# Local attention on Trainium2: scores of one head on half of TensorE's rows, softmax maxima for two pairs at once in two PSUM banks, and a ring of four banks for the rest

## The chip, the cores and the metric

The kernel runs on one core of a Trainium2 chip. A core has TensorE (PE in the profile, with its weight loads as PEld), VectorE (DVE), ScalarE (ACT), GpSimd (POOL) and SyncE (SP), which here issues the DMAs. Each engine has its own queue and takes its instructions in the order in which they were issued to it; the engines meet through semaphores. TensorE writes its results to PSUM, which this kernel divides into eight banks of 128 partitions x 512 float32 values; VectorE and ScalarE read and write PSUM and SBUF.

The metric is device microseconds of one launch. The kernel before took 4397.36 us (median of three runs, 4397.0 to 4401.22).

## The reference, cut to what matters

The program is a chain of eight layers on 8 sequences of 256 tokens with 128 features: a selective state space model, a local transformer block, an attention over tokens, the same local block a second time, a linear attention, a four-bit feed-forward, a head attention and the four-bit feed-forward again. The change lies in the local block alone, which runs twice. It has six layers (DEPTH = 6), and each has an attention and a feed-forward part with residual additions:

```python
HEADS, DIM_HEAD, WINDOW = 16, 64, 32
def attn_layer(x, Wqkv, qs, ksc, Wo):
    q, k, v = (sh(t) for t in split(x @ Wqkv, 3))       # (b, 16 heads, 256, 64)
    q, k = l2norm(q) * qs, l2norm(k) * ksc
    q = q * cos * scale + rotate_half(q) * sin * scale
    k = k * cos / scale + rotate_half(k) * sin / scale
    # a window of 32 queries sees its own 32 keys and the 32 before
    sim  = einsum('bhwie,bhwje->bhwij', bq, look(bk)) * 8.0
    sim  = where(mask, -finfo.max, sim)                 # 32 x 64 per window
    attn = softmax(sim, -1)
    out  = einsum('bhwij,bhwje->bhwie', attn, look(bv))
    return out @ Wo
def ffn_layer(x, g, bln, W1, b1, W2, b2):
    a, gate = split((layernorm(x) * g + bln) @ W1 + b1, 2)
    return (a * gelu(gate)) @ W2 + b2
```

All of it is float32.

## The kernel before, in words

The data are worked on transposed (features on partitions) in four chunks `c` of two sequences, so 512 tokens at a time. A chunk in a layer is a unit; six layers of four chunks make 24 units, and the 16 heads of a unit go as eight pairs `p` = 0 to 7. `LocalBlock.steps` (L607) writes the whole order by hand: one step `i` for each pair of each unit, and in a step one call for each stage, some for a later pair and some for an earlier one. No scheduler changes it. The stages of a step, in the order in which they are issued to every engine's queue:

- `rotate` (pair i+6): two GpSimd operations of 128x1024, L367 and L368; the first waits for the DMA that swaps the halves of a head.
- `prep` (pair i+1): a matmul spreads the key norms over the partitions (L410), and VectorE multiplies keys by them into a buffer `kb` (L414), twice, once for each head of the pair, with a column `hcol` that is one on the rows of that head and zero on those of the other.
- `share` (pair i-1, odd pairs only): VectorE's softmax sums of two pairs and their reciprocals (L460, L461).
- `project` (pair i+7): six matmuls make q and k in two PSUM banks (L213 to L215); ScalarE copies each bank out (L338), VectorE multiplies it by a table (L340) after ScalarE's read of the same bank, two DMAs from SP's queue swap the halves (L343, L344), ScalarE squares (L348).
- `rounded`, `shared` (GpSimd, L469: probabilities times reciprocals), then side work (weight loads of the next layer: `load_qk`, `load_v`, `load_1`), `norms` and `norms_end` (VectorE L377, three ScalarE operations L131 to L134, VectorE L142 and L146), and a piece of `feed`, the feed-forward of the unit one and a half units behind: eight pieces, at pairs 4 to 7 the layer norm, at 0 the gate, at 2 the other half, at 3 the output matmuls (L563).
- `attended`, `turn` (odd pairs: transposes of the probabilities into two banks, L482, copied by ScalarE, L485).
- `scores` (pair i): 16 matmuls (L429), then four VectorE operations on the bank (L437 to L440): times the query norms, plus the mask, the maxima, and the subtraction into SBUF.
- `values` (32 matmuls, L325, into two banks, copied by ScalarE, L327), `attend` (odd pairs, L505), `squares` (L359), and last `soft` (odd pairs: ScalarE's exponential of two pairs at once, L450).

In the program a float32 matmul is one call; the trace shows most of them as two instructions, each with a weight load of its own.

A row block of 128 holds both heads of a pair, first halves of both, then second halves (rows 0 to 31 are head 0, 32 to 63 head 1, 64 to 95 head 0, 96 to 127 head 1). So a score matmul runs over all 128 rows and makes both heads' scores side by side, 2 x 64 columns, from the two masked copies in `kb`. The four windows of a group go to four column tiles of 32, that is, to four blocks of 32 output partitions.

PSUM banks are given out in turn. `K.bank` (L121) takes the next bank of a named list, and whoever gets a bank again waits for the last reader of its former contents:

```python
RING, NRM, ACC = "012345", "6", "7"      # L38
```

The ring of six serves `prep` (one bank), `project` (two), `scores` (one), `values` (two), `turn` (two in odd steps), the feed-forward (ten in a unit), `attended`, `rounded` and the weight loads.

Of the kernel before, what the change touches and what calls it, by code (L numbers as in the profile page):

```python
# [10 lines left out]
F32 = mybir.dt.float32  # L11
# [10 lines left out]
NCH = 4  # L22
CT = 512
# [14 lines left out]
RING, NRM, ACC = "012345", "6", "7"  # L38
# [5 lines left out]
def f32(ap):  # L44
    return ap.bitcast(F32)
# [172 lines left out]
class LocalBlock:  # L218


    def __init__(self, k):
# [5 lines left out]
        self.mask = k.const(P, "c_mask", (128, 512), BF)  # L227
        self.hcol = k.const(P, "c_hcol", (128, 2))
# [9 lines left out]
        self.zero = P.tile([32, 128], BF, name="zero")  # L238
        self.kb = [P.tile([128, 2, 32 + CT], F32, name="kb_%d" % i) for i in range(NKB)]
# [12 lines left out]
        for t in self.rs:  # L252
            nc.vector.tensor_scalar(t, self.mask, 0.0, None, ALU.mult)
# [75 lines left out]
    def project(self, u, p):  # L329
# [13 lines left out]
        nc.sync.dma_start(out=sw[0:64], in_=raw[64:128])  # L343
        nc.sync.dma_start(out=sw[64:128], in_=raw[0:64])  # L344
# [61 lines left out]
    def prep(self, u, p):  # L406
# [6 lines left out]
        for h in range(2):  # L413
            nc.vector.scalar_tensor_tensor(kb[:, h, 32:], tt[:, 1], self.hcol[:, h:h + 1], rb, ALU.mult, ALU.mult)  # L414
        u.kb[p] = kb

    def scores(self, u, p):


        k, P, nc = self.k, self.P, self.k.nc  # L420
        mm = nc.tensor.matmul
        kb = u.kb.pop(p)
        qf = u.t.pop(p)[:, 0]
        sp = k.bank(RING)
        s4 = sp.rearrange("p (o a j) -> p a o j", o=2, a=8)
        for wg in range(4):
            for w in range(4):
                win = 4 * wg + w
                mm(s4[32 * w:32 * w + 32, 2 * wg:2 * wg + 2], qf[:, 32 * win:32 * win + 32],  # L429
                   kb[:, :, 32 * win:32 * win + 64].rearrange("p h (o j) -> p h o j", o=2),  # L430
                   start=True, stop=True)
        mx = P.tile([128, 8], F32, name="mx", tag="mx", bufs=2)
        if p % 2 == 0:
            u.pr = P.tile([128, 2, 8, 2, 32], F32, name="pr", tag="pr", bufs=NPR)
        pr = u.pr
        rq = u.rq[p // GP][:, p % GP].rearrange("p w h -> p (w h)")
# [5 lines left out]
        if p % 2:  # L442
            u.prs[p] = pr
# [1052 lines left out]
```

## Time and profile before

| what | value |
|---|---|
| median of three runs | 4397.36 us |
| the profiled execution | 4402.16 us, span 4400.4 us, mean granted TensorE clock 0.922 |
| first and last score matmul of the first local block | 630.2 us to about 2195 us |
| the same of the second | 2435 us to about 4015 us |
| score matmuls L429 | 12288 instructions, 418.6 us busy, mean 277 ns |
| VectorE on the scores, L437 to L440 | 4 x 384 operations of 128x512, 694, 700, 691 and 691 ns |
| VectorE, keys times norms, L414 | 768 operations of 128x512, 741 ns |
| ScalarE, exponential L450 | 192 operations of 128x1024, 1061 ns |
| SP's swap DMAs, L343 and L344 | 768 of 256 KB, median 3.5 us from issue to landing |

The span is the time from the first to the last instruction of the profiled execution, and busy time is the union of an engine's instructions. [...] An "idle before" figure is the time for which the engine stood still ahead of a group of instructions, with the operation that ended it.

In the trace one can follow the steps by the first score matmul of each. In a unit in which no weights are loaded, one step after the other takes 5.88, 10.07, 9.84, 8.06, 6.39, 8.77, 6.27 and 8.80 us, 64.1 us in all, the same to 0.05 us from layer to layer. The three other units of a layer take about 66, 69 and 66 us.

### The profile page before, as it was taken

How to read it: one execution, taken by the hardware profiler on the slowest of the kernel's cores; microseconds unless marked ns; L12 is line 12 of the kernel's file. 1: busy time of each engine (PE TensorE's matmuls, PEld its weight loads, DVE VectorE, ACT ScalarE, POOL GpSimd, SP SyncE). 2: the span in 40 equal slices, each digit the busy share in tenths (PEclk: the TensorE clock that was granted, in tenths of full speed). 3: DMA queues.
4: the chain of work that ended last, by engine and by line, in shares of the span. 5: the costliest groups of instructions: out<-in, count | busy, mean ns of one | idle time of the engine just before them, and what ended most of it. 6: DMA issues, size and time to landing. Idle time of an engine off the chain costs nothing.

```text
span 4400.4 us, 147972 instructions
## 1 busy us (share of the span) xinstructions
PE 3760.2 (85%) x64201; PEld 2852.7 (65%) x64201; DVE 3705.8 (84%) x5687; ACT 2645.0 (60%) x5050; POOL 3078.2 (70%) x1546
## 2 busy tenths in 40 slices
PE   5656679999999999999966899999999999997376
PEld 2222257777778778777744777787787777775144
DVE  6999958888888888888876788888888888887988
ACT  5423347767667677677544676676676767764322
POOL 3656668878778778787575887787877877862433
PEclk7777889999999999999966999999999999998578
DMA  0000033323233233333202332232333323221000
GB/s 19 7 3 16 1 78 81 89 74 89 72 75 90 73 85 74 78 82 76 54 20 68 81 90 72 69 93 72 88 74 74 87 71 92 72 71 42 15 6 10
DMA packets 134900, 272.97 MB, mean 62 GB/s; under 512 B 31020, under 2 KB 68328, under 8 KB 134248
## 3 DMA queue, kind: packets, MB, share of 16 engines
q1 hardware_dynamic: 134248, 263.51, 23.9%
q8 instruction: 503, 8.24, 0.8%
q14 instruction: 149, 1.22, 0.1%
HBM read 49.50 MB, written 6.29 MB: 13 GB/s over the span
## 4 chain that ended last, share of the span: by engine, by line
DVE 38%; PE 37%; ACT 13%; issue 8%; POOL 2%; DMA 2%; SPq 0%; DVEq 0%; POOLq 0%; ACTq 0%
PE pb L505 6%; PE pb L325 5%; DVE big L340 4%; DVE big L816 4%; DVE big L414 4%; PE pb L429 3%; DVE big L460 3%; PE pb L563 3%; PE pb L359 3%; DVE pb L438 2%; DVE big L439 2%; PE pb L410 2%; DVE pb L437 2%; DVE big L440 2%; ACT big L348 2%
## 5 line engine op out<-in xcount | busy, mean ns | idle before, releaser
L367 POOL TENSOR_TENSOR big<-big 128x1024 f32<-128x1024 f32 x384 | 916.0, 2385 | 405.0 <-DMA big<-big 319.7
L368 POOL TENSOR_TENSOR big<-big 128x1024 f32<-128x1024 f32 x384 | 917.2, 2389 | 30.1
L325 PE MATMUL pb<-big 128*32 128x128 f32 x24576 | 748.8, 274 | 4.3 <-DVE big L301 4.0
L414 DVE SCALAR_TENSOR_TENSOR big<-big,pb 128x512 f32<-128x512 f32 x768 | 537.7, 741 | 193.7 <-PE pb L410 153.3
L325 PEld LDWEIGHTS pb<-big 128*32 128x32 f32 x24576 | 681.6, 111 | 12.9 <-DVE big L301 7.1
L327 ACT COPY big<-pb 128x512 f32<-128x512 f32 x768 | 439.1, 597 | 317.8 <-PE pb L325 316.0
L338 ACT COPY big<-pb 128x512 f32<-128x512 f32 x768 | 440.1, 585 | 280.3 <-PE pb L215 248.6
L340 DVE TENSOR_TENSOR big<-pb,big 128x512 f32<-128x512 f32 x768 | 482.6, 668 | 43.6 <-ACT big L338 43.0
L469 POOL TENSOR_TENSOR big<-big 128x1024 f32<-128x1024 f32 x192 | 365.6, 1904 | 217.2 <-ACT big L348 133.6
L348 ACT ACTIVATE big<-big 128x512 f32<-128x512 f32 x768 | 443.4, 629 | 0.0
L505 PE MATMUL pb<-big 128*32 128x128 f32 x11520 | 402.0, 278 | 43.8 <-ACT big L485 35.0
L817 POOL TENSOR_TENSOR big<-big 128x1024 f32<-128x1024 f32 x128 | 305.3, 2398 | 191.4 <-DVE big L816 186.3
L213 PE MATMUL pb<-bigr 128*128 128x512 f32 (+1 forms) x1056 | 429.6, 407 | 11.3 <-ACT bigr L298 8.9
L215 PE MATMUL pb<-bigr 128*128 128x512 f32 (+1 forms) x1056 | 422.0, 400 | 4.2 <-DVE bigr L299 3.7
L429 PE MATMUL pb<-big 128*32 128x128 f32 x12288 | 418.6, 277 | 7.7 <-DVE big L440 4.7
L214 PE MATMUL pb<-bigr 128*128 128x512 f32 (+1 forms) x1056 | 420.1, 398 | 1.0 <-POOL bigr L203 1.0
L505 PEld LDWEIGHTS pb<-big 128*32 128x32 f32 x11520 | 325.3, 111 | 107.2 <-ACT big L485 91.4
L429 PEld LDWEIGHTS pb<-big 128*32 128x32 f32 x12288 | 314.9, 110 | 110.0 <-ACT big L338 32.7
L810 PE MATMUL pb<-bigr 128*128 128x512 f32 x512 | 214.0, 533 | 181.2 <-DVE big L816 124.6
L437 DVE TENSOR_TENSOR pb<-pb,big 128x512 f32<-128x512 f32 x384 | 266.4, 694 | 69.7 <-PE pb L429 67.3
L450 ACT ACTIVATE big<-big 128x1024 f32<-128x1024 f32 x192 | 203.7, 1061 | 191.5 <-DVE big L440 179.1
L359 PE MATMUL pb<-big 128*32 128x128 f32 x6144 | 296.4, 275 | 19.2 <-DVE big L146 8.6
(270 smaller groups left out, 7400.6 us busy)
## 6 DMA issues: line engine op xcount, KB each, us to landing
big<-big SPq DMA_DIRECT2D x768, 256.0 KB, 3.5
big<-in_wqk SPq DMA_DIRECT2D x96, 128.0 KB, 3.4
big<-x SPq DMA_DIRECT2D x28, 256.0 KB, 2.8
big<-in_c_rot SPq DMA_DIRECT2D x24, 256.0 KB, 4.9
big<-in_wv SPq DMA_DIRECT2D x48, 128.0 KB, 3.9
big<-in_wo SPq DMA_DIRECT2D x48, 128.0 KB, 3.3
big<-big SPq DMA_DIRECT2D x384, 16.0 KB, 2.4
x<-big SPq DMA_DIRECT2D x20, 256.0 KB, 3.9
```

The costliest lines, as they stand in the source:

```text
L213: mm(out, w[:, 0], x[:, 0], start=start, stop=False)
L325: nc.tensor.matmul(vp[32 * h:32 * h + 32, bass.ts(w, 128)], xw, wv[:, bass.ts(h, 128)], start=True, stop=True)
L327: nc.scalar.copy(v2[:, 4 * q:4 * q + 4].rearrange("p w f -> p (w f)"), vp)
L338: nc.scalar.copy(raw[:, s], ps)
L340: nc.vector.tensor_tensor(tt[:, s].rearrange("p (b t) -> p b t", b=2), ps.rearrange("p (b t) -> p b t", b=2), ct, ALU.mult)
L348: nc.scalar.activation(sq, raw[:, s], AF.Square)
L359: self.k.nc.tensor.matmul(u.nrm[32 * i:32 * i + 32, 0:128], self.sel[:, j, pl], q[:, bass.ts(i, 128)], start=(pl == 0 and j == 0), stop=(p ...
L367: nc.gpsimd.tensor_tensor(s4, s4, u.w.tab[1][:, :, None, :].broadcast_to([128, 2, 2, T]), ALU.mult)
L368: nc.gpsimd.tensor_tensor(tt, tt, sw, ALU.add)
L414: nc.vector.scalar_tensor_tensor(kb[:, h, 32:], tt[:, 1], self.hcol[:, h:h + 1], rb, ALU.mult, ALU.mult)
L429: mm(s4[32 * w:32 * w + 32, 2 * wg:2 * wg + 2], qf[:, 32 * win:32 * win + 32], kb[:, :, 32 * win:32 * win + 64].rearrange("p h (o j) -> p ...
L505: mm(u.acc[32 * w:32 * w + 32, bass.ts(wg, 128)], pts[o][:, 32 * win:32 * win + 32], v2[:, win - 1 + o], start=False, stop=(g == 3 and o = ...
```

## The change

The rows of a pair are put in another order by the host's layout of the weights: head 0 has rows 0 to 63, head 1 rows 64 to 127. From that follows:

- `scores` makes a matmul for each head: 32 instead of 16, each over 64 rows and 64 columns, with the two heads on the two halves of TensorE's rows. Head 0 writes to bank 4, head 1 to bank 5, and the two pairs of an even and an odd step stand side by side in them.
- The four VectorE operations go into a new stage `maxima`, issued after `scores` in odd steps only, on 128x1024 in two banks. `soft` has two exponentials of 128x512, which also put the probabilities in the old order.
- `prep` has one VectorE multiplication instead of two, and `kb` holds one copy; `hcol` goes.
- The ring has four banks (0 to 3); banks 4 and 5 belong to the scores.
- The swap takes four DMAs of 32 rows instead of two of 64.
- `load_1` makes its rounded weights with two ScalarE operations and a GpSimd subtraction instead of one ScalarE and one VectorE operation (L298, L299), and starts three steps earlier; `share` is issued after `project` and `rounded`.

```diff
-RING, NRM, ACC = "012345", "6", "7"
+RING, SCO, NRM, ACC = "0123", "4", "6", "7"
...
-            hl = P.tile([128, 2, m], F32R, name="w1hl", tag="w1", bufs=7)
-            nc.scalar.activation(hl[:, 0], r, AF.Copy, scale=self.ffc[:, l, 0:1])
-            nc.vector.scalar_tensor_tensor(hl[:, 1], r, self.ffc[:, l, 0:1], f32(hl[:, 0]), ALU.mult, ALU.subtract)
-            w.w1[i] = hl
+            nc.scalar.activation(r, r, AF.Copy, scale=self.ffc[:, l, 0:1])
+            w.w1[i] = k.split(P, r, (128, m), "w1", 7, self.top)
...
-        nc.sync.dma_start(out=sw[0:64], in_=raw[64:128])
-        nc.sync.dma_start(out=sw[64:128], in_=raw[0:64])
+        for a in range(4):
+            b = a ^ 1
+            nc.sync.dma_start(out=sw[32 * a:32 * a + 32], in_=raw[32 * b:32 * b + 32])
...
-        for h in range(2):
-            nc.vector.scalar_tensor_tensor(kb[:, h, 32:], tt[:, 1], self.hcol[:, h:h + 1], rb, ALU.mult, ALU.mult)
+        nc.vector.tensor_tensor(kb[:, 32:], tt[:, 1], rb, ALU.mult)
...
-        sp = k.bank(RING)
-        s4 = sp.rearrange("p (o a j) -> p a o j", o=2, a=8)
+        if p % 2 == 0:
+            u.sp = k.bank(SCO, 2)
         for wg in range(4):
             for w in range(4):
                 win = 4 * wg + w
-                mm(s4[32 * w:32 * w + 32, 2 * wg:2 * wg + 2], qf[:, 32 * win:32 * win + 32],
-                   kb[:, :, 32 * win:32 * win + 64].rearrange("p h (o j) -> p h o j", o=2),
-                   start=True, stop=True)
...
+                for h in range(2):
+                    o, rows = CT * h + 256 * (p % 2) + 64 * wg, slice(64 * h, 64 * h + 64)
+                    nc.tensor.matmul(u.sp[32 * w:32 * w + 32, o:o + 64], qf[rows, 32 * win:32 * win + 32],
+                                     kb[rows, 32 * win:32 * win + 64], start=True, stop=True)
...
+    def maxima(self, u, p):
...
+        if p % 2 == 0:
+            return
+        sp, rq = u.sp, u.rq[p // GP][:, p % GP - 1:p % GP + 1].rearrange("p l w h -> p h (l w)")
+        s4 = sp.rearrange("p (h c j) -> p h c j", h=2, c=8)
+        g16 = lambda t: t.rearrange("p (g j) -> p g j", g=16)
+        nc.vector.tensor_tensor(s4, s4, rq[:, :, :, None].broadcast_to([128, 2, 8, 64]), ALU.mult)
+        s4 = sp.rearrange("p (a c) -> p a c", a=4)
+        nc.vector.tensor_tensor(s4, s4, self.mask[:, None].broadcast_to([128, 4, 256]), ALU.add)
+        mx = P.tile([128, 16], F32, name="mx", tag="mx", bufs=2)
+        nc.vector.tensor_reduce(mx, g16(sp), AX.X, ALU.max)
+        ps = u.prs[p] = P.tile([128, 2 * CT], F32, name="ps", tag="ps", bufs=1)
+        nc.vector.tensor_tensor(g16(ps), g16(sp), mx[:, :, None].broadcast_to([128, 16, 64]), ALU.subtract)
...
-        prf = u.prs[p].rearrange("p o a h j -> p (o a h j)")
-        self.k.nc.scalar.activation(prf, prf, AF.Exp)
+        ps = u.prs.pop(p).rearrange("p (g w o j) -> p o g w j", g=4, w=4, o=2)
+        pr = u.pr[p] = self.P.tile([128, 2, 4, 4, 32], F32, name="pr", tag="pr", bufs=NPR)
+        for o in range(2):
+            self.k.nc.scalar.activation(pr[:, o].rearrange("p w g j -> p g w j"), ps[:, o], AF.Exp)
...
-            do(self.share, -1)
             u, p = do(self.project, 7)
             do(self.rounded, 5)
+            do(self.share, -1)
...
+                if p == 4 and u.c == NCH - 1 and not last:
+                    side.append(self.load_1(ws[u.l + 1], u.l + 1))
...
             do(self.scores, 0)
+            do(self.maxima, 0)
```

More of the change, by code (lines that the diff above doesn't have):

```diff
@@ L237, in __init__ @@
         self.b1 = k.const(P, "b1", (128, DEPTH, 6))
-        self.zero = P.tile([32, 128], BF, name="zero")
-        self.kb = [P.tile([128, 2, 32 + CT], F32, name="kb_%d" % i) for i in range(NKB)]
+        self.zero = P.tile([32, 512 + 128], BF, name="zero")
+        self.kb = [P.tile([128, 32 + CT], F32, name="kb_%d" % i) for i in range(NKB)]
         self.y = [P.tile([128, 2, 257], F32, name="y_%d" % c) for c in range(NCH)]
@@ L644, in steps @@
                     if u.c == NCH - 1 and not last:
-                        side += [self.load_1(ws[u.l + 1], u.l + 1), self.load_2(ws[u.l + 1], u.l + 1)]
+                        side.append(self.load_2(ws[u.l + 1], u.l + 1))
                     if last:
@@ L1430, in layout @@
     d["w2"] = i["L0_ffn_W2"]
-    row = np.array([(r // 64) * 32 + r % 32 for r in range(128)])
-    swp = np.array([(1 - r // 64) * 32 + r % 32 for r in range(128)])
+    row = np.arange(128) % 64
+    swp = (row + 32) % 64
     qs, ks = i["L0_ffn_q_scale"], i["L0_ffn_k_scale"]
```

48 lines of the change are left out of this document (16 added, 32 removed).

## Prediction, made before the changed kernel ran

> **What bounds the kernel now.** I read the busy tenths over time first, then the busy time of each engine over the two local blocks, TensorE's waits in one layer, the costliest groups, and last the timeline of single steps. The two stretches that hold the changed work (us, then busy time and instructions of PE, PEld, DVE, ACT and POOL, the clock, the DMA share, GB/s):
>
> ```profile
> 630.00:2194.00 1564.00, 1491.97 (x30286) 1211.89 (x30285) 1344.97 (x2143) 1085.49 (x2050) 1208.38 (x599) 1.00 0.32 78
> 2435.00:4014.00 1579.00, 1498.11 (x30289) 1216.99 (x30290) 1350.74 (x2146) 1087.58 (x2051) 1207.82 (x600) 0.99 0.31 78
> ```
>
> TensorE is busy 95% of 3143 us, at full clock; VectorE 86%, GpSimd 77%, ScalarE 69%. In the steps, TensorE's instructions follow each other without a gap but for the waits below: TensorE is the bound, and VectorE is second by a small distance. TensorE's own waits in one layer (874.3 to 1138 us, four units), us and times:
>
> ```profile
> PE pb L563 <- DVE big L440: 2.2, 2, 1.1
> PE pb L505 <- ACT big L485: 2.1, 3, 1.0
> PE pb L283 <- DVE big L460: 1.3, 1, 1.3
> PE pb L296 <- DVE big L414: 1.0, 1, 1.0
> PE pb L296 <- DVE big L440: 0.9, 1, 0.9
> ...
> ```
>
> All of that answer's rows are 9.2 us of 264. Most are waits for a bank of the ring: L563 gets the bank of the scores, which VectorE gives back with L440. A unit without weight loads waits 1.8 us in its 64.1 (L563 1.1, L505 0.5, L482 0.2). The groups (busy, mean ns, idle before):
>
> ```profile
> L414 DVE SCALAR_TENSOR_TENSOR big<-big,pb 128x512 f32<-128x512 f32 x768 | 537.7, 741 | 193.7 <-PE pb L410 153.3
> L429 PE MATMUL pb<-big 128*32 128x128 f32 x12288 | 418.6, 277 | 7.7 <-DVE big L440 4.7
> L450 ACT ACTIVATE big<-big 128x1024 f32<-128x1024 f32 x192 | 203.7, 1061 | 191.5 <-DVE big L440 179.1
> ```
>
> The last row matters most: ScalarE stands still 179 us in front of the exponential, until VectorE has ended the scores, and whatever ScalarE has to do next stands behind it. The timeline around pair 1 of a unit shows the chain (start, us):
>
> ```profile
> 953.06 1.08 PE L429 MATMUL pb<-big 128*32 128x128 f32 x32
> ...
> 955.42 0.29 DVE L142 TENSOR_TENSOR big<-pb,big 128x128 f32<-128x128 f32 x1 [1.01 <-ACT big L134]
> ...
> 955.95 0.69 DVE L437 TENSOR_TENSOR pb<-pb,big 128x512 f32<-128x512 f32 x1
> ...
> 958.13 0.69 DVE L440 TENSOR_TENSOR big<-pb,big 128x512 f32<-128x512 f32 x1
> ...
> 958.92 1.06 ACT L450 ACTIVATE big<-big 128x1024 f32<-128x1024 f32 x1
> ...
> 959.89 1.15 ACT L338 COPY big<-pb 128x512 f32<-128x512 f32 x2
> ```
>
> Scores, VectorE 2.9 us, exponential, then the next step's copies of q and k out of PSUM. With six banks TensorE is not held by it.
>
> **The change, part by part.**
>
> *Score matmuls.* A group of 32 instructions takes 0.90 us until the values start (953.06 to 953.96). On the four column tiles:
>
> ```profile
> 1511.91 0.32 PE L429 MATMUL pb<-big 128*32 128x128 f32 x4
> 1517.04 0.43 PE L167 MATMUL pb<-big 128*32 128x128 f32 x8
> 4287.91 1.00 PE L1306 MATMUL pb<-big 128*128 128x64 f32 x8
> ```
>
> Four on four tiles span 0.32 us where one lasts 0.27 to 0.30, so starts are at most some 16 ns apart; a round of four then takes 0.11 us (1.08 less 0.27, over seven rounds). The change makes 64 instructions of half the columns on eight tiles, again eight rounds. No row shows two halves of the rows at work together. Lower end: half the columns, half the round, 8 x 0.055 = 0.45 us. Upper end: 0.9 us, from L1306, whose 64 columns still follow each other at 0.10 to 0.11 us, or from halves that go in turn. I take 0.47, because streaming sets the round in the nearest row (L429, same weights of 32 columns; L1306 loads 128). To it comes 0.1 us in each step: the weight loads stand 0.20 us ("issue") where the tiles change shape, half of it beyond the last matmul, and now values follow scores with another shape. So 0.57 for 0.90: 0.33 us less in a step, 2.6 in a unit.
>
> [...]
>
> *VectorE.* Two L414 (1.40 us) become one of about 0.65. Four operations of 0.69 to 0.70 in each step become four of 128x1024 in each odd step; L814, the same form in PSUM, takes 1.22, so 5.0 us with the gaps, against 2 x 2.9. Together 1.1 us less in a step. VectorE is not the bound; what counts is that the block of 5.0 us lies ahead of the exponential where 2.9 lay. Nothing is saved by its being idle more.
>
> *ScalarE.* Two exponentials of 0.6 for one of 1.06: 0.1 us more in a step pair, on the chain.
>
> *The ring.* The scores take their bank out of it, but a bank comes round after four requests instead of six. I went through a plain unit step by step with the durations above (L410 0.35, project 1.4, turn 1.0, values 1.75, attend and squares 2.3 or 0.55, gate and half 2.1, L563 2.7, key multiplication 0.65, copy 0.55, table multiplication 0.65, which starts after ScalarE's copy). New waits:
> - Step 2, whose feed takes three banks. At pair 1 VectorE starts 2.9 us after the first score matmul (the norm chain ending in L142, L146) and ends 7.9 after it; the next key multiplication ends at 8.55. TensorE, through values, attend, squares, L410 and project, wants that bank at 7.0: 1.5 us. The next bank needs exponential (9.1), copy (9.65), table (10.3); TensorE is there at 9.25: 1.0. Then 0.2 for the bank of `rounded`. Sum 2.7.
> - Step 0: maxima of pair 7 start 0.8 after the scores (no norms), table multiplication done at 8.2, TensorE there at 7.75: 0.5. The second values bank is that of the first gate matmul, released by the first gelu at 11.1 (squares, then a table load of 1.28): 0.6.
> - Step 1: attend waits for ScalarE's copies, 0.5, as before.
> - Step 5: the second values bank is that of the variance, held until the Newton step at the end of `mid`: 0.9.
> - Step 6: the layer norm's bank needs the key multiplication behind the maxima: 0.6.
> Sum 5.8, of which 0.6 swallows gaps of shape changes that TensorE had anyway: 5.2. The unit: 64.1 - 1.8 - 2.6 + 5.2 = 64.9. That the new waits together are as large as the matmul saving and the old waits is the heart of this forecast.
>
> *The swap.* SP takes 0.46 + 0.54 us for two DMAs, so up to 1.1 us more for four; all of that or nothing, if half the rows take half the time. GpSimd's L367 starts that much later. It waits on the DMA anyway (319.7 us in 150 waits), idles 23% of a step of 8.2 us (1.9 us), and its result is used five steps on: nothing. Without the idle it would be 1.1 us a step.
>
> *load_1.* 72 L299 (1.13 us median, slow beside GpSimd) leave VectorE; the waits of L296 above are part of the 9.2. GpSimd gets 72 subtractions, between half of L203's 0.73 us and all of it, in its idle time. ScalarE gets six more of 0.39 us at each of ten layer changes, 23 us, half of it ahead of a norm chain: +12. `share` behind `project`: releases the q and k banks 1.4 us earlier in even steps (in the times above); the sums come later, but GpSimd's 1.9 us still end before the turn of the next step.
>
> *Sum.* A layer is four units: 4 x (5.2 - 2.6) - 9.2 = +1.2 us; twelve layers +14, with load_1 +26. The profiled execution took 4402.2 (span 4400.4 and 1.8 around it): 4428; it lies 4.8 above the median of the runs, so 4423.
>
> **Rivals.**
> - *Faster: the ring of four keeps up.* If the new waits are half of mine, a layer has 4 x (2.6 - 2.6) - 9.2, twelve give -110, with +12: 4402 - 98 - 5 = 4299. For it: TensorE is the bound by every view, matmul time goes away, and VectorE and L563's waits get relief. It decides from the point where the maxima at pair 1 start soon after the scores (0.8 instead of 2.9 us). Against it: the wait for L134 stands in the timeline.
> - *Slower: the halves of the rows take turns.* Scores 0.9 + 0.1: 0.43 us more a step than forecast, half of it inside waits: 83 to 165 us, 4506 to 4588. It decides from a round of 0.08 us on. For it: L1306. Against it: the spacing on column tiles.
> - *Slower: GpSimd falls behind the four DMAs.* In the steps with weight loads, where GpSimd has more to do: 10 layer changes x 8 steps x 0.55 us = 44 us, 4467.
> - *Nothing:* waits and saving within 9 us of each other; part of the forecast.
>
> **How the numbers follow.** Forecast (waits within a third of mine, some 4380 to 4470) 0.50; ring keeps up 0.28; turns 0.14; GpSimd 0.08. A measurement of this kernel can tell 0.2%, 9 us. Of the forecast's half, 0.06 is faster by more, 0.09 within, 0.35 slower. Faster 0.28 + 0.06 = 0.34, same 0.09, slower 0.35 + 0.14 + 0.08 = 0.57. The range leaves out a tenth on each side: down to 4310, near the full rival, and up to 4530, inside the turns. The likeliest case alone: 4380 to 4470.
>
> **What the new profile would show.** Right: score groups of 64 in about 0.7 us with the last one's own 0.25; VectorE 80% or less in the local blocks; TensorE's waits 20 us or so in a layer, on the key and table multiplications and the gelu; plain units near 65 us. Wrong: score groups near 1.1 us (turns), waits under 12 us a layer (ring keeps up), GpSimd's waits on DMAs doubled.

## The result, and the profile after

The changed kernel takes 4570.07 us (median of four runs, 4555.8 to 4574.39) against 4398.29 us for the kernel before on the same chip: a ratio of 1.0384, 95% interval 1.036 to 1.0408. It is 172 us slower. The prediction was 4423 us with a range up to 4530: the sign was right, the size was not.

The profiled execution took 4568.33 us, span 4566.5 us (before: 4400.4), mean granted TensorE clock 0.910 (0.922). From the first to the last score matmul the two local blocks now take 1651 us each, 87 and 70 us more than before; all the rest of the program together differs by 10 us. The stretches of the two blocks, with the columns of the prediction's first fence (us, busy time and instructions of PE, PEld, DVE, ACT and POOL, clock, DMA share, GB/s):

```profile
630.00:2280.00 1650.00, 1513.03 (x36387) 1197.36 (x36374) 1143.91 (x1537) 1086.28 (x2176) 1218.30 (x629) 0.98 0.32 75
2528.00:4179.00 1651.00, 1518.84 (x36463) 1202.30 (x36461) 1145.85 (x1543) 1086.83 (x2177) 1218.44 (x630) 0.98 0.32 75
```

VectorE's work fell from 2696 to 2290 us, as the change meant it to, and that bought nothing. TensorE is still the busiest engine, but it now stands still for 3301 - 3032 = 269 us in the blocks, where it stood 3143 - 2990 = 153: 116 us of the 158 us that these stretches grew by. The other 42 us are in busy time, although the score matmuls became cheaper; the clock column, 0.98 for 1.00 and 0.99, says why, and the clock has a part of its own below. Where TensorE waits is seen in one layer (894.5 to 1174.5 us; us in total, times, longest):

```profile
PE pb L213 <- DVE big L337: 4.5, 6, 1.5
PE pb L322 <- DVE big L146: 3.8, 4, 1.7
PE pb L213 <- DVE big L411: 2.2, 2, 1.1
PE pb L179 <- DVE big L337: 2.1, 2, 1.4
...
PE pb L282 <- DVE big L411: 1.4, 2, 1.1
PE pb L295 <- DVE big L411: 1.4, 2, 1.1
```

All rows of that answer make 19.5 us, against 9.2 before. In this layer the waits for the scores' bank (L440 in the old lines) are gone; over the run 15.6 us of them are left (L427 below). In their place stand waits for a ring bank whose reader is the key multiplication (L411), the table multiplication (L337) or the Newton step (L146). The groups say the same of the engines (busy, mean ns, idle before):

```profile
L337 DVE TENSOR_TENSOR big<-pb,big 128x512 f32<-128x512 f32 x768 | 509.9, 688 | 373.6 <-ACT big L335 373.4
...
L453 ACT ACTIVATE big<-big 128x512 f32<-128x512 f32 x384 | 221.1, 623 | 525.9 <-DVE big L444 512.4
...
L427 PE MATMUL pb<-big 64*32 64x64 f32 x24576 | 336.2, 228 | 15.8 <-DVE big L444 15.6
L427 PEld LDWEIGHTS pb<-big 64*32 64x32 f32 x24576 | 273.1, 107 | 120.9 <-issue 94.7
```

ScalarE stands 512 us in front of the exponential (179 before), and VectorE 373 us in front of the table multiplication, waiting for ScalarE's copy of the same bank (43 before). The two engines wait for each other in turn. The timeline around pair 1 of a plain unit, put in order of time:

```profile
900.60 0.86 PE L427 MATMUL pb<-big 64*32 64x64 f32 x64
901.39 1.95 PE L322 MATMUL pb<-big 128*32 128x128 f32 x64
...
903.47 1.23 DVE L438 TENSOR_TENSOR pb<-pb,big 128x1024 f32<-128x1024 f32 x1
...
907.26 1.22 DVE L444 TENSOR_TENSOR big<-pb,big 128x1024 f32<-128x1024 f32 x1
908.40 0.68 DVE L411 TENSOR_TENSOR big<-big,pb 128x512 f32<-128x512 f32 x1
908.57 1.15 ACT L453 ACTIVATE big<-big 128x512 f32<-128x512 f32 x2 [2.27 <-DVE big L444]
909.13 0.50 PE L213 MATMUL pb<-bigr 128*128 128x512 f32 x1 [1.10 <-DVE big L411]
909.63 1.05 ACT L335 COPY big<-pb 128x512 f32<-128x512 f32 x2
910.23 1.29 DVE L337 TENSOR_TENSOR big<-pb,big 128x512 f32<-128x512 f32 x2 [1.16 <-ACT big L335]
910.97 0.50 PE L213 MATMUL pb<-bigr 128*128 128x512 f32 x1 [0.88 <-DVE big L337]
```

One chain runs through it: maxima from 903.47 to 908.48, then the key multiplication, which frees TensorE's first bank; beside it the exponentials, behind them the copy, then the table multiplication, which frees the second. The brackets of the two L213, 1.10 and 0.88 us, are what TensorE pays in this step.

### The profile page after: what moved, and what is told of

It is laid out like the page before. It is cut to its first block, busy times and chain, and to the rows that moved or that the text cites. A ratio compares the mean times of both kernels' runs of the same rounds, so it can differ in the third digit from the quotient of the medians.

```text
span 4566.5 us, 172806 instructions
## 1 busy us (share of the span) xinstructions
PE 3822.6 (84%) x76489; PEld 2829.7 (62%) x76489; DVE 3293.2 (72%) x4463; ACT 2648.2 (58%) x5313; POOL 3101.9 (68%) x1618
## 5 line engine op out<-in xcount | busy, mean ns | idle before, releaser
L322 PE MATMUL pb<-big 128*32 128x128 f32 x24576 | 775.5, 276 | 43.7 <-DVE big L146 39.6
L337 DVE TENSOR_TENSOR big<-pb,big 128x512 f32<-128x512 f32 x768 | 509.9, 688 | 373.6 <-ACT big L335 373.4
L322 PEld LDWEIGHTS pb<-big 128*32 128x32 f32 x24576 | 649.5, 111 | 105.9 <-DVE big L146 51.5
L324 ACT COPY big<-pb 128x512 f32<-128x512 f32 x768 | 438.8, 594 | 323.7 <-PE pb L322 322.8
L411 DVE TENSOR_TENSOR big<-big,pb 128x512 f32<-128x512 f32 x384 | 262.4, 683 | 407.3 <-PE pb L408 405.1
L335 ACT COPY big<-pb 128x512 f32<-128x512 f32 x768 | 425.4, 582 | 181.1 <-PE pb L215 114.5
L453 ACT ACTIVATE big<-big 128x512 f32<-128x512 f32 x384 | 221.1, 623 | 525.9 <-DVE big L444 512.4
L213 PE MATMUL pb<-bigr 128*128 128x512 f32 (+1 forms) x1056 | 444.6, 421 | 78.7 <-DVE big L337 45.9
L346 ACT ACTIVATE big<-big 128x512 f32<-128x512 f32 x768 | 444.2, 631 | 0.0
L215 PE MATMUL pb<-bigr 128*128 128x512 f32 (+1 forms) x1056 | 434.3, 411 | 0.0
L214 PE MATMUL pb<-bigr 128*128 128x512 f32 (+1 forms) x1056 | 432.4, 409 | 0.9 <-POOL bigr L203 0.9
L505 PE MATMUL pb<-big 128*32 128x128 f32 x11520 | 397.0, 277 | 22.6 <-ACT big L485 9.9
L505 PEld LDWEIGHTS pb<-big 128*32 128x32 f32 x11520 | 331.9, 110 | 70.7 <-ACT big L485 46.3
L427 PE MATMUL pb<-big 64*32 64x64 f32 x24576 | 336.2, 228 | 15.8 <-DVE big L444 15.6
L427 PEld LDWEIGHTS pb<-big 64*32 64x32 f32 x24576 | 273.1, 107 | 120.9 <-issue 94.7
L357 PE MATMUL pb<-big 128*32 128x128 f32 x6144 | 299.1, 274 | 18.7 <-DVE big L146 9.0
L203 POOL TENSOR_TENSOR bigr<-big,bigr 128x512 fp32r<-128x512 f32 (+3 forms) x264 | 223.1, 850 | 119.5 <-ACT bigr L202 119.1
```

The costliest lines, as they stand in the source:

```text
L213: mm(out, w[:, 0], x[:, 0], start=start, stop=False)
L214: mm(out, w[:, 0], x[:, 1], start=False, stop=False)
L215: mm(out, w[:, 1], x[:, 0], start=False, stop=stop)
L322: nc.tensor.matmul(vp[32 * h:32 * h + 32, bass.ts(w, 128)], xw, wv[:, bass.ts(h, 128)], start=True, stop=True)
L324: nc.scalar.copy(v2[:, 4 * q:4 * q + 4].rearrange("p w f -> p (w f)"), vp)
L335: nc.scalar.copy(raw[:, s], ps)
```

## Theories and experiments

Theory A is the prediction's: the ring of four is a little too short, and the rest of the change is small. The rivals: B, the maxima of two pairs in one block of 5 us are what makes the banks late; C, the exponentials ahead of ScalarE's copies are; R, the ring of four does it whatever stands on VectorE; T, the row halves take turns. Each kernel is compared with the kernel before, run on the same chip (4397 to 4399 us).

### Is it the ring?

The kernel before with a ring of four, its scores in turn in two banks of their own:

```diff
-RING, NRM, ACC = "012345", "6", "7"
+RING, SCO, NRM, ACC = "0123", "45", "6", "7"
...
-        sp = k.bank(RING)
+        sp = k.bank(SCO)
```

> The kernel before with only the ring changed: four banks in the ring, the scores of a pair in one of two banks of their own, in turn; score matmuls, VectorE's four operations of 128x512 in each step, key products and swaps as before. Theory A (the block of four 128x1024 operations ahead of the exponential is what the four banks can't cover): the block is still 2.9 us, L563 no longer waits for the scores' bank (1.1 us a unit), so within 40 us of before: 4360 to 4440. Rival R (four banks alone are too few, whatever stands ahead of the exponential): most of the 4.6 us a unit of new waits, 4500 to 4600.

4524.02 us, ratio 1.0285 (1.0268 to 1.0302): 126 us slower, as rival R had it. The split alone, without the wide block, costs most of what the change lost. TensorE's waits over the run:

```profile
PE pb L213 <- DVE big L340: 75.9, 81, 1.7
PE pb L482 <- DVE big L414: 42.1, 65, 1.5
PE pb L325 <- DVE big L146: 40.7, 44, 1.6
PE pb L179 <- DVE big L340: 23.9, 20, 1.6
```

They are the waits of the changed kernel at the old lines. The 42.1 us are for the old key multiplication, two operations (1.41 us) that stand behind the 2.9 us of the maxima in each step. So R is right where VectorE has its old work. The next run shows that it does not hold with the new.

### Is it the block of two pairs?

The changed kernel with the four VectorE operations in each step again, on 128x512 in halves of the two banks; all else as changed:

```diff
-        if p % 2 == 0:
-            return
...
+        e = p % 2
...
+        cut = lambda t: t.rearrange("p (h e c j) -> p h e c j", h=2, e=2, c=4)[:, :, e]
+        s4 = cut(u.sp)
...
+        nc.vector.tensor_tensor(cut(u.ps), s4, mx[:, :, :, None].broadcast_to([128, 2, 4, 64]), ALU.subtract)
```

> The changed kernel with the four VectorE operations in each step on the pair's own half (128x512 in two banks of 256 columns) instead of 128x1024 in odd steps; all else as changed. Theory A: at pair 1 the block ends 2.1 us earlier, the waits on the key product and the table product at pairs 0, 2 and 6 go (3 to 4 us a unit, of 48 units): 4400 to 4460. Rival R: the ring is the same, so 4540 to 4580.

4385.0 us, ratio 0.9964 (0.9949 to 0.9979): 185 us faster than the changed kernel and 13 faster than before, below what either expectation had. VectorE does more work than in the changed kernel, and the same four banks go round. VectorE at pair 1:

```profile
897.54 0.69 DVE L437 TENSOR_TENSOR pb<-pb,big 128x512 f32<-128x512 f32 x1
...
899.73 0.69 DVE L446 TENSOR_TENSOR big<-pb,big 128x512 f32<-128x512 f32 x1
900.71 0.69 DVE L411 TENSOR_TENSOR big<-big,pb 128x512 f32<-128x512 f32 x1 [0.29 <-PE pb L408]
902.17 1.29 DVE L337 TENSOR_TENSOR big<-pb,big 128x512 f32<-128x512 f32 x2 [0.77 <-ACT big L335]
```

The maxima end after 2.9 us, and now VectorE waits for TensorE's L408 and not the other way round. TensorE waits 1.2 us in that unit instead of 3.9. Theory B holds in this: without the block of 5 us the loss is gone, on the same short ring. In the two blocks TensorE stands still 109 us less, and 54 us less are lost to its clock (worked out as in the last section). Whether the block does its harm through the key multiplication behind it or through the exponentials that wait for it, this run can't tell; the runs with later exponentials below separate the two in part.

Taken with the run before, a ring of four stands a block of 2.9 us followed by one key multiplication, but neither 2.9 us followed by two nor 5.0 us followed by one. That it is the second key multiplication which sinks the split alone is not shown: the two kernels also differ in the score matmuls, the first feed-forward weights, the swap and the shares. With the weights as before, the short block takes 4405.7 us (below), still 118 us under the split alone, and the cheaper score matmuls account for some 42 of these. The split with one key multiplication and nothing else was not run.

### Are six banks better, then?

The same kernel, the scores' two banks taken out of a ring of six in each step:

```diff
-RING, SCO, NRM, ACC = "0123", "4", "6", "7"
+RING, NRM, ACC = "012345", "6", "7"
...
-        if p % 2 == 0:
-            u.sp = k.bank(SCO, 2)
+        if k.turn[RING] == 4:
+            k.bank(RING)
+        u.sp = k.bank(RING, 2)
+        k.bank(RING)
...
```

> The kernel with maxima in each step (4385), but with the two banks of the scores taken out of a ring of six in each step, as the kernel before takes its one. If the fixed split into four and two banks is still what costs there (waits of 3.4 us in the units with weights, 1.2 in the plain ones): 4330 to 4365. If two banks per step out of six leave the others no more room than four did: 4375 to 4400. If the two banks are held so long that the ring runs dry: 4420 or more.

4474.16 us, ratio 1.0176 (1.016 to 1.0191): 89 us slower than with the split. One row explains most of it:

```profile
PE pb L213 <- DVE big L448: 126.3, 121, 3.8
```

L448 is the last reader of the scores. Two banks held until the maxima have ended come round among the others, and the projection and the feed-forward run into them. So the split into four and two is the better use of the banks here, and of the three cases expected the last one came. The form that was run needs two neighbouring banks and passes one over where it finds none, so a ring of six with single banks is not judged by it.

### Are the exponentials in the way?

The changed kernel, the exponentials issued in the next step behind the projection's copies:

```diff
             do(self.rounded, 5)
+            do(self.soft, -1)
             do(self.share, -1)
...
-            do(self.soft, 0)
```

> The changed kernel (4570) with one move: the two exponentials of a pair of pairs are issued one step later on ScalarE, behind the projection's copies and the rounded norms, ahead of the sums of the exponentials. Theory B: the loss sits on VectorE, where the key multiplication and the first table multiplication stand behind the 5.0 us block of the maxima. The exponentials only wait for that block themselves, so moving them frees ScalarE's copies, but the table multiplications read the same bank after their VectorE queue, and TensorE's waits stay: 4545 to 4580. Rival C: the 1.2 us of exponentials ahead of the first projection copy (the copy starts 0.5 us after the key multiplication has ended) make the second wait after pair 1 (0.88 us in a plain unit, waiting for the table multiplication). Then that wait goes in most odd steps, some 1 to 1.5 us per unit: 4495 to 4525.

4512.6 us, ratio 1.0265 (1.0247 to 1.0282): 58 us faster than the changed kernel, in the range of rival C. The waits of TensorE for L337 after the copies leave the list, and VectorE gets a new one, at the sum of the shares right behind the exponentials: 271.6 us in 183 waits. But the two blocks, in the columns of the first fence, show that the gain is hardly what C names:

```profile
627.00:2249.00 1622.00, 1492.02 (x36462) 1187.22 (x36461) 1150.26 (x1538) 1096.69 (x2178) 1217.63 (x629) 0.99 0.33 76
2493.00:4118.00 1625.00, 1494.29 (x36455) 1187.79 (x36452) 1151.85 (x1543) 1095.80 (x2176) 1216.86 (x630) 0.99 0.33 76
```

TensorE still stands still for 3247 - 2986 = 261 us, 8 less than in the changed kernel: other waits took the place of those for L337. What went is time lost to the clock, 22 us instead of 70. That the waits are packed less closely is a reading; the last section has the stretches that a halved clock followed.

So the sums and products were put behind the feed-forward as well:

```diff
-            do(self.share, -1)
-            do(self.shared, -1)
+            do(self.soft, -1)
...
+            do(self.share, -1)
+            do(self.shared, -1)
             do(self.attended, -3)
...
-            do(self.soft, 0)
```

> The changed kernel (4570) with both of these moves. With the exponentials alone moved it took 4513 while VectorE stood 272 us at the share's sum. If the exponentials' place is a good part of the loss and the sum's wait has eaten some of the gain: 4440 to 4500. If the block of 5 us is the whole of the rest and the sum's wait lay in time that VectorE had to spare: 4500 to 4525.

4469.22 us, ratio 1.0162 (1.0147 to 1.0177): 101 us of the change's 172 us come back by the order of two engines' queues alone, with the block of 5 us in place. The first of the two expectations holds: with the exponentials and sums out of the way, the block hurts much less. In the blocks TensorE stands still 234 us (269 in the changed kernel) and loses 24 us to the clock (70). The block's 185 us and these 101 us are not two separate sums: the order of the queues behind the block takes over half of its harm away, and without the block the same moves gain nothing, as the next runs show.

The same two moves on the kernel with maxima in each step, one after the other:

> The kernel with maxima in each step (4385) with the same move of the exponentials. Theory B: with the short block there is little left to win, waits 1.2 us in a plain unit: 4375 to 4400. Rival C: the exponentials still hold the first copy in odd steps, and 0.3 to 0.7 us per unit goes: 4350 to 4372.

> The kernel with maxima in each step (4385), exponentials one step later behind the rounded norms (as in the run at 4639), and now the sums and products of the shares later too, ahead of the transpose of the values' result and not straight behind the exponentials, where VectorE stood for 323 us waiting for them. If that wait made the 4639 and the move itself is harmless: 4360 to 4400. If the buffer that the exponentials read (the subtraction of the next step writes it again) or the later shares cost as much by themselves: 4450 or more, with waits for the share's product ahead of the transposes.

4639.19 us (ratio 1.0547, 1.0532 to 1.0563) and 4553.6 us (1.0356, 1.0341 to 1.0372): worse than the 4385.0 without them. The first ran against everything expected of it; the second had its time from the second expectation, but the reason given there only in part: the transposes wait 44 us for the shares' product, but 88 us for the key multiplication. VectorE's longest wait in the first kernel, and TensorE's longest in the local blocks of the second:

```profile
DVE big L463 <- ACT big L455: 322.9, 180, 3.6
```

```profile
PE pb L484 <- DVE big L411: 88.3, 85, 2.3
```

VectorE stands at the sum (L463) in even steps, behind it come that step's maxima, and the next key multiplication is late for the transposes (L484). In the paired form an even step has no maxima, and the same wait lies in idle time. One move, two signs: by these rows it depends on what is queued behind the waiting instruction. That is a reading and not a full account: moving the sums brought back 86 of 254 us, and VectorE still waits 186.6 us at the sum in the second kernel.

The block can also be cut: inverse norms and mask in the odd step, maximum and subtraction behind the next key multiplication, exponentials late as in the first of these runs:

```diff
             do(self.prep, 1)
+            do(self.maxima_end, -1)
...
+            do(self.soft, -1)
...
-            do(self.soft, 0)
```

> The changed kernel (4570) with the maxima of two pairs still as four operations of 1024 columns, but cut: inverse norms and mask in the odd step, maximum and subtraction in the next step behind the key multiplication and ahead of the table multiplications, and the exponentials behind the rounded norms as in the run before. VectorE does the same work. Theory B (the length of the piece that stands ahead of the key multiplication): the wait for the key multiplication goes, but the table multiplications now stand behind 2.5 us, which they wait for as well: 4420 to 4500. Rival W (it is the work per step, or the two banks held longer, and not the place): 4550 to 4600.

4622.2 us, ratio 1.0511 (1.0496 to 1.0527): slower than all the paired forms, and above both expected ranges. The piece behind the key multiplication now stands ahead of the table multiplications, and the next scores wait for their two banks:

```profile
PE pb L213 <- DVE big L337: 97.9, 72, 2.2
PE pb L427 <- DVE big L450: 89.9, 73, 5.4
```

This was meant to help theory B and did not: by the first row, cutting the block only moved the late piece to the next reader in the queue, and by the second, rival W had a part of the reason, banks held longer.

### What do the score matmuls cost?

The prediction had 0.57 us for a group. In the timeline above it is 901.39 - 900.60 = 0.79. The recorded starts of a group show two paces (medians over 384 groups): the first 32 start 6.9 ns apart within an eight, eight in some 0.06 us, so the halves of the rows do work side by side; then comes a gap of 0.09 us, and after it one starts every 11 ns on the average (8.4 in the middle of that stretch). First to last start is 0.643 us; 0.146 us follow until the values. Taking the halves in turn is the test of the first reading:

```diff
-        for wg in range(4):
-            for w in range(4):
-                win = 4 * wg + w
-                for h in range(2):
+        for h in range(2):
+            for wg in range(4):
+                for w in range(4):
+                    win = 4 * wg + w
```

> The changed kernel with its 32 score matmuls in another order: all 16 of head 0 (rows 0 to 63), then all 16 of head 1, so that no two halves of the rows have work at once but at the border. If the halves work side by side in the changed kernel, a group grows from 0.79 us until the values start to 1.0 or more, 0.2 us and up in 384 steps, some of it in waits: 4600 to 4680. If they took turns all along, nothing changes: 4555 to 4580.

4588.98 us, ratio 1.0434 (1.0416 to 1.0452): 19 us more than the changed kernel, between the two expected ranges; a group takes 0.92 us. The halves do overlap when they are issued in alternation: 32 starts take 0.238 us there, where the first 16 of one half alone take 0.212. But the order is worth only 0.13 us a step, since the second part of a group goes at 11 to 12 ns a start in both orders. To see what limits it, each group of the kernel with maxima in each step was cut in two around the first bank of values:

```diff
-            do(self.scores, 0)
-            do(self.maxima, 0)
-            u, p = do(self.values, 2)
+            do(self.scores, 0, 0)
+            do(self.values, 2, 0)
+            do(self.scores, 0, 1)
+            do(self.maxima, 0)
+            u, p = do(self.values, 2, 1)
```

> The kernel with maxima in each step (4385), with each score group of 64 matmuls cut into two of 32, one ahead of and one behind the first bank of values. In the changed kernel the first 32 to 36 matmuls of a group start every 6.9 ns, then there is a gap of 0.09 us and the rest starts every 8.4 ns: 0.79 us where 0.57 was predicted. Theory Q: that is the supply of instructions (128 short ones in 0.64 us, a stock that has built up before the group is used up); then both halves run at 6.9 ns without a gap, 0.22 us each and 0.1 to 0.15 us more for a change of tile shape: 0.65 to 0.75 us for both, and 4365 to 4400 in all. Rival S: the gap and the slower pace belong to the tiles or banks of the second half (its columns of the bank, or the change of shape); then the second half alone is still slow, with the change of shape paid twice: 0.9 us or more for both and 4410 to 4450.

```profile
903.18 0.46 PE L427 MATMUL pb<-big 64*32 64x64 f32 x32
903.75 1.08 PE L322 MATMUL pb<-big 128*32 128x128 f32 x32
904.76 0.45 PE L427 MATMUL pb<-big 64*32 64x64 f32 x32
905.14 1.08 PE L322 MATMUL pb<-big 128*32 128x128 f32 x32
```

Both halves now run at the first pace: 0.238 us from first to last start (median of 764 groups), 0.384 to the values. So neither the second half's tiles nor its banks are slow: 32 matmuls and their 32 weight loads go at the predicted pace, and what comes after them in one go does not. The prediction's 0.47 us would be right, 2 x 0.238, if the first pace lasted. That it is the supply of instructions that gives out (theory Q) fits these rows and is not shown. The time, 4413.66 us (ratio 1.004, 1.0025 to 1.0055), is 28 us more than uncut, above what theory Q gave and in rival S's range, though S had the pace wrong: the 0.146 us between a last start and the values pass twice, and the maxima start a bank later (VectorE waits 253.5 us for the scores instead of 82.4).

### The small parts

The swap in four DMAs on the kernel before:

```diff
-        nc.sync.dma_start(out=sw[0:64], in_=raw[64:128])
-        nc.sync.dma_start(out=sw[64:128], in_=raw[0:64])
+        for a in range(4):
+            b = a ^ 2
+            nc.sync.dma_start(out=sw[32 * a:32 * a + 32], in_=raw[32 * b:32 * b + 32])
```

> The kernel before with its swap as four DMAs of 32 rows instead of two of 64. If GpSimd's lag behind the swap DMAs were part of the loss: 4430 or more, with more waits of L367 on DMAs. Theory A, where the result is wanted five steps later: no change, 4390 to 4406, and SP's issues take up to 1.1 us more a step.

4413.97 us, ratio 1.0041 (1.0028 to 1.0055): 15 us, between the two expected ranges. A plain unit stays at 64.1 us; the loss lies in the units where SP also issues weight loads. There TensorE waits 15.6 us for the DMAs of one of the weights (`in_wo`) instead of 4.7, while GpSimd's waits for the swap did not grow (301 us in 133 waits, 320 in 150 before). By these rows it is the weights that come later from the same queue, and not GpSimd that falls behind.

The earlier weights and the later sum of the shares, together on the kernel before, then each alone:

> The kernel before (4398) with only two moves of the change: the first feedforward weights split on ScalarE and GpSimd and loaded three steps earlier, and the sum of the shares behind the projection's copies. The prediction counted 12 us for the weights and nothing for the shares: 4405 to 4415. If the weights cost nothing here because they run beside TensorE: 4393 to 4402. If one of the two is a hidden gain: 4375 to 4393.

> The kernel before (4398) with the sum of the shares alone moved behind the projection's copies and the rounded norms. Both moves together took 44 us away, where the prediction had put 12 us for the weights and nothing for the sum. If the sum of the shares is the gain (VectorE no longer stands at it, waiting for the exponential, ahead of the key multiplication and the table multiplications): 4350 to 4370. If the weights are the gain: 4390 to 4402.

> The other half: the kernel before with the first feedforward weights alone in their new form and three steps earlier. The prediction's 12 us of loss: 4405 to 4415. If they are the gain of 44 us: 4350 to 4375. If nothing: 4393 to 4402.

Together 4353.87 us (ratio 0.99, 0.9885 to 0.9915); the shares alone 4402.6 (1.0009, 1.0 to 1.0019), hardly to be told from nothing; the weights alone 4343.52 us, ratio 0.9879 (0.9863 to 0.9896). A part that the prediction counted as 12 us of loss gains 54 us, and the kernel before with that part alone is the fastest of all that were run:

```diff
-            hl = P.tile([128, 2, m], F32R, name="w1hl", tag="w1", bufs=7)
-            nc.scalar.activation(hl[:, 0], r, AF.Copy, scale=self.ffc[:, l, 0:1])
-            nc.vector.scalar_tensor_tensor(hl[:, 1], r, self.ffc[:, l, 0:1], f32(hl[:, 0]), ALU.mult, ALU.subtract)
-            w.w1[i] = hl
+            nc.scalar.activation(r, r, AF.Copy, scale=self.ffc[:, l, 0:1])
+            w.w1[i] = k.split(P, r, (128, m), "w1", 7, self.top)
...
+                if p == 4 and u.c == NCH - 1 and not last:
+                    side.append(self.load_1(ws[u.l + 1], u.l + 1))
...
-                        side += [self.load_1(ws[u.l + 1], u.l + 1), self.load_2(ws[u.l + 1], u.l + 1)]
+                        side.append(self.load_2(ws[u.l + 1], u.l + 1))
```

> The kernel before with the first feedforward weights three steps earlier, but split on ScalarE and VectorE as before. With the new form too it took 4343.5, 54 us less. If the time is the gain (the weights' loads, copies and bias products no longer meet those of the value weights and the feedforward of the same two units): 4343 to 4360. If the form is the gain (no VectorE operation that waits for ScalarE and GpSimd in those units): 4385 to 4402. Between them: both.

The earlier time with the old form takes 4390.68 us, ratio 0.9984 (0.9975 to 0.9994): 7 us. The other 47 us come with the form. TensorE's waits in the two blocks of the kernel before:

```profile
PE pb L505 <- ACT big L485: 34.7, 49, 1.4
...
PE pb L213 <- ACT bigr L298: 8.9, 10, 0.9
PE pb L296 <- DVE big L440: 8.6, 10, 0.9
...
PE pb L215 <- DVE bigr L299: 3.7, 8, 0.5
```

and of the kernel with the new weights:

```profile
PE pb L503 <- ACT big L483: 17.7, 37, 0.8
...
PE pb L296 <- DVE big L438: 4.7, 10, 0.5
```

Half of the first wait (the copy L485 is L483 there) and the matmuls' waits for L298 and L299 are no longer in the list. In all, TensorE stands still 106 us in the blocks instead of 153, and loses 8 us to the clock instead of 15. The old VectorE operation waits for ScalarE's copy (16.7 us in 19 waits), and the bias sum and all that follows on VectorE stand behind it; the new subtraction waits on GpSimd's queue, off that path. That this queueing is the whole of the 47 us is argued from these rows, not shown; the new form at the old time was not run.

On the kernel with maxima in each step the old weights were put back:

> The kernel with maxima in each step (4385) with the first feedforward weights loaded and split as in the kernel before. If the new form costs the 12 us of the prediction: 4368 to 4378. If it costs nothing: 4380 to 4390. If the earlier load is what keeps the weights out of the way of the four swaps: 4392 to 4405.

4405.7 us, ratio 1.0016 (1.0006 to 1.0026): 21 us more, so the gain is there too, but smaller.

## Why the prediction was wrong

Two terms of the sum failed: the score matmuls, which were priced too low, and the clock, which was put at nothing without a reason.

- **The bound: right.** TensorE sets the time; VectorE's 406 us less in the blocks bought nothing.
- **Score matmuls: the first term that failed.** 0.57 us a group was predicted, 0.79 measured. The mechanism held (halves side by side, eight matmuls in 0.06 us, as taken); the sum failed because it took that pace for all 64, where it lasts for 32, and 0.1 us for the shape where 0.146 passes. A unit gains 0.9 us instead of 2.6; over 384 steps of 0.22 us that is 84 us of the 147 between 4423 and 4570.
- **VectorE and ScalarE: right.** 69% in the blocks (80% or less predicted), 1.22 to 1.23 us for 128x1024, 0.68 for the key multiplication, 0.62 for the half exponential.
- **The ring: near, and partly by luck.** After pair 1 the waits are 1.10 and 0.88 us where 1.5 and 1.0 were worked out, at step 5 0.95 where 0.9 was; the gelu's wait did not show. A plain unit waits 3.9 us where 5.8 was worked out. The layer's 19.5 us meet the 20 of the forecast because the units with weight loads, which the walk left out, wait more. Measured from first score matmul to first score matmul, the units of this layer take 66.4, 70.9, 71.5 and 71.3 us, where they took 64.1, 66.3, 68.7 and 65.9 and the plain one was forecast at 64.9. What the walk through one unit could not show is how unsteady that balance is: 185 us hang on the length of one VectorE block, 101 us on where the exponentials and shares stand.
- **The clock: the second term that failed.** The prediction read full clock off the kernel before and kept it. By the last section 55 us more are lost to a halved clock after waits. With the scores' 84 us that makes 139 of the 147. That the other misses come to 8 together is a difference and not a measurement: the waits in the blocks grew by 116 us where 48 x 5.2 - 12 x 9.2 = 139 was forecast, the rest of the program by 10 us where nothing was, and no run separates what remains.
- **The swap: wrong by a little.** Nothing was predicted, 15 us measured. The GpSimd rival had the right units, those with weight loads, but the wrong engine and three times the price.
- **load_1: wrong sign.** +12 us predicted, -54 measured on the kernel before, -21 on the kernel with maxima in each step. The step priced ScalarE's extra 0.39 us operations and let VectorE's L299 go for nothing, since VectorE is not the bound. What L299 waited for, and what was queued behind it, was left out.
- **The rivals.** "The halves take turns" named 4506 to 4588, which holds the result by luck, for a reason that the starts refute. "The ring keeps up" is what happens with the short block, by far not to 4299.

The single parts do not add up: -54 (weights), +5 (shares), +15 (swap), -42 (scores, 0.11 us in 384 steps), +126 (ring) and +185 (block) make 235, not 172, and the single key multiplication has no run of its own. The parts share their waits: the ring was priced with two key multiplications, and the weights' gain shrinks in the new kernel.

## What to carry to other kernels

Before two short operations on one engine are merged into a long one, look at what is queued behind them and who waits for it: VectorE's total work fell by 15% here, and the merged block still cost 185 us: banks were given back later, and 70 us were lost to the clock where the short block lost 16. When banks are few, the order of the readers on the other engines is worth more than the matmuls were: one move of two stages gave 101 us in one form of this kernel and cost 169 in the other. So try the small moves of such a change each by itself, as the one that seemed to cost was the gain. And price a burst of very short matmuls by a row that is as long as the burst: here the pace broke after 32 matmuls with their 32 loads, from 6.9 ns a start to 11 on the average. Last, look at the granted clock when a change puts waits close together.

## What the runs showed of the hardware

**Some waits were paid twice.** In the units with weight loads two waits followed each other closely, and then the matmuls ran at half pace (timeline of the changed kernel):

```profile
974.10 0.27 PE L399 MATMUL pb<-big 128*128 128x128 f32 x1
975.48 0.38 PE L295 MATMUL pb<-big 128*128 128x1 f32 x2 [1.11 <-DVE big L411]
977.32 0.80 PE L213 MATMUL pb<-bigr 128*128 128x512 f32 x1 [1.46 <-DVE big L337]
977.91 0.63 PE L214 MATMUL pb<-bigr 128*128 128x512 f32 x1
...
980.64 0.39 PE L215 MATMUL pb<-bigr 128*85 128x512 f32 x1
```

From 977.91 to 980.05 the starts are 0.43 us apart, where 0.23 is usual. Summed over the two blocks, one minus the granted clock times the length of the stretch, 70 us are lost to the clock in the changed kernel, 15 in the kernel before and 16 with maxima in each step. That is 55 us that no list of waits shows. The length of a wait alone does not tell it: 1.46 after 1.11 us was followed by a halved clock, 0.82 after 1.11 us at 1048 was too, and 0.88 after 1.10 us in the timeline at the top was not. In the trace's record every change of the granted clock lies on one grid of 3.413 us. The stretches of that grid around the three pairs of waits (us, busy time and instructions of PE, clock, DMA share, GB/s):

```profile
973.47:976.88 3.41, 1.28 (x7) 1.00 0.05 12
976.88:980.29 3.41, 2.97 (x7) 0.50 0.57 130
1045.15:1048.56 3.41, 1.48 (x7) 1.00 0.00 0
1048.56:1051.97 3.41, 3.41 (x35) 0.50 0.73 167
908.61:912.03 3.42, 2.02 (x8) 1.00 0.06 13
```

TensorE stood still for 2.1 and 1.9 us in the two stretches ahead of a halved one, and for 1.4 us in the third, whose waits the grid cuts at 908.61. So it goes through the blocks of the changed kernel (650 to 2180 and 2560 to 4160 us): all 26 stretches at full clock with over 1.71 us of standing still, half of the 3.41, were followed by a halved one, none with under 1.23 us was, and of the 34 between 1.23 and 1.71 ten were. In the kernel before, one stretch with 1.77 us was not. These rows tell what the halved stretches followed; what sets the clock is not shown.

**Two halves of the rows worked side by side**: from first to last start, 32 matmuls on both halves in alternation took 0.238 us, the first 16 on one half alone 0.212. 64 matmuls of 64 columns on eight tiles took 2 x 0.238 us from first to last start when they came in two groups of 32, and 0.643 us in one.
